# First attention and first mixture of experts: two steps of the sort a gap, the last sequence turned later, row fetches sent from an earlier step

## The chip, the cores and the metric

The kernel runs on one NeuronCore of one Trainium2 chip. The metric is the device time of one execution in microseconds (us), and the median over several executions is what counts. A profile of one execution gives the start and end of every instruction on the five engines (PE for matmuls, DVE for vector work, ACT for activations, POOL for GpSimd, SP for issuing transfers), and of every packet that the DMA engines moved.

## What is computed

The input is x with 8 sequences of 256 tokens and 256 features. Four layers follow each other, each an attention and a feed-forward part, and after each part x becomes layernorm(x + part(x)). Only the first layer matters here:

```python
def L0_attn(x):                       # 16 heads of 16, keys and values of 4 heads
    q, k, v = rope(x @ wq), rope(x @ wk), x @ wv
    return softmax(causal(q @ k.T / 4)) @ v @ wo

def L0_ffn(x):                        # 32 experts in 4 groups
    scores = sigmoid(x @ gate_w.T)
    two groups per token by the sum of their two best (scores + bias)
    the 8 best experts inside these two groups, weights scaled to sum 2.5
    h = relu((x @ fc1_w.T) @ w1[e].T) ** 2
    routed = sum over e of weight[e] * (h @ w2[e].T), then @ fc2_w.T
    shared = relu(x @ shared_up_w.T) ** 2 @ shared_down_w.T
    return shared + routed
```

Everything is float32 except a few 0/1 and mask operands in bf16.

## The kernel before, in words

The phases follow each other: attn0, ffn0, attn1 and so on. In attn0 and ffn0 the author writes the order of the instructions by hand: each engine's queue holds them in the order in which the Python generators issue them, apart from some that the recording layer of the manual schedule moves by a few places. [...]

**attn0** goes over the sequences b = 0 to 7. For each one it has three "gaps", i = 0, 1, 2: `maxima(b + 1)` makes a piece of the next sequence's scores (L331, mask L339) and takes their maxima on DVE (L343); `weights(b)` makes the transposed scores (L374, L382), ACT takes the exponentials (L388), and POOL clears the upper triangle of the diagonal blocks with an affine select (L390). After each of these comes a `fill(k, n)`. It runs what is ready beside the scores: pieces of `finish` (values L405, copy L410, transposes L416, division L420 and L421, transposes L431, copy L435, output projection L440, residual L164, statistics L183 and L184, reciprocal root on POOL L146 and L147, normalising L190), n pieces of the queue `ahead` (from b = 5 on the shared expert of token blocks 0 and 1, `ffn0_shared`, L1075 and L1088), and at its end one step of the queue `sorting`. `norm_done(b)` calls `transpose_x(b)` (L154), which turns the normalised X[b] into the block xT that all later matmuls read.

**The sort**, `ffn0_sort`, runs once for sequences 0 to 3 (group 0) and once for 4 to 7 (group 1). It is a generator of 23 steps and then 16 scatters. Step 1 to 3 gate and latent matmuls (L991, copies L995 on DVE and L996 on ACT), 4 sigmoid, 5 to 8 the best of each group (L1016), 9 the group choice (L1019 to L1022), 10 the one-hot `r_one` (L877, L879), 12 counting matmuls (L893) and their sums (L896 to L902), 13 and 14 slots, 15 and 17 which expert each tile has (L942, L944), 18 to 21 the best 8 experts (L230 to L235), 22 the weights, 23 their copy into the latent rows `lat` (L1054, L1060). Each scatter is one indirect transfer issued by POOL (L953), which writes 128 rows of 136 values to the table `lrows` in DRAM. POOL takes about a microsecond for each.

**ffn0** runs `ffn0_shared` for block 2 (sequences 4 and 5): eight steps, i = 0 to 3 for the four up-projections (two matmuls of 512 columns each, L1075), i = 4 to 7 for the down-projections (L1088). In its loop stand two sort steps per i, the turning of the last sequence, X[7], at i = 1, the start of group 1's sort at i = 4, and at i = 6 the first step of `ffn0_experts` and `then()`, which sends for the 6 MB of weights of attn1 on SP. `ffn0_experts` takes 19 tiles of 128 sorted rows. `fetch(j)` sends for the rows of tiles j and j + 1 (SP, L1110), `turn(j)` sends for the rows of tiles j + 4 and j + 5 if j is even, copies the tile's expert weights on POOL (`wc`, L1121) and transposes the rows (L1126, copy L1128 on ACT), `up` and `down` are the two matmul groups (L1134, L1151), with the weighted sum on DVE (L1160, L1162). During these tiles group 1's sort runs one step per half tile. The combine of group 0 and the tiles of group 1 follow in the same way, beside the shared expert of block 3.

PSUM has two buffers per tag (a, s, t, o). SBUF that attn0 used is given to ffn0 (weights `w2`, relu and hs, `wc`, `xg`) once attn0's last matmul has read it.

Of the kernel before, what the change touches and what calls it, by code (L numbers as in the profile page):

```python
# [19 lines left out]
NB = 8  # L20
# [19 lines left out]
class Model:  # L40
# [209 lines left out]
    def attn0(self, w, act, start=False, beside=None, between=()):  # L250
# [100 lines left out]
        def spread(b):  # L351

            pt = self.psum.tile([P, 2, P], BF16, tag="t", name="ps_tb")
            for qc in range(2):
                nc.tensor.transpose(
                    pt[:, qc, :], HLs[b % 2][:, qc].rearrange("p s r -> p (s r)"), self.identb
                )
            e = act.tile([P, 2, 4, P], BF16, tag="E", name="E")
            nc.vector.tensor_tensor(
                e,  # L360
                pt.unsqueeze(2).to_broadcast([P, 2, 4, P]),
                w["delta"].unsqueeze(1).unsqueeze(3).to_broadcast([P, 2, 4, P]),
                ALU.mult,
            )
            E[b] = e
# [96 lines left out]
        ends, ahead, sorting = [], [], []  # L462

        def step(queue):
            while queue:
                if next(queue[0], queue) is not queue:
                    return
                queue.pop(0)

        def fill(k, n):  # L470


            if k in (0, 2):
                for x in ends[-1:]:
                    next(x)
            if k == 0 and len(ends) > 1:
                next(ends.pop(0))
            for _ in range(n):
                step(ahead)
            if k in (3, 5):  # L480
                for x in ends[-1:]:
                    next(x)
            step(sorting)

        for _ in project(0):
            pass
# [5 lines left out]
        for b in range(NB):  # L492
            nxt = None
            if (b == 0 or b % 2 == 1) and (b + 3) // 2 < NBLK:
                ahead.append(project((b + 3) // 2))
            if b + 1 < NB:
                nxt = maxima(b + 1)
            if b == 0:
                steps = (3, 1, 1, 1, 1, 2)
            elif b % 2 == 1 and b < NB - 3:  # L500
                steps = (0, 2, 0, 1, 1, 1)
            elif b < NB - 3:
                steps = (0, 1, 0, 1, 1, 1)
            else:
                steps = (0, 1, 1, 1, 1, 1)
            if b == NB - 3:
                ahead.extend(between)
                if beside:
                    sorting.append(beside)
            mine = weights(b)  # L510
            for i in range(3):
                if nxt is not None:
                    next(nxt)
                if b > 1 and i == 1:
                    self.norm_done(b - 2)
                fill(2 * i, steps[2 * i])
                next(mine)
                if i == 2 and nxt is not None:
                    next(nxt, None)
                fill(2 * i + 1, steps[2 * i + 1])  # L520
            if nxt is not None:
                spread(b + 1)
            ends.append(finish(b))
# [574 lines left out]
    def ffn0_experts(self, w1, w2, g, act):  # L1098


        nc = self.nc
        rows, outs, expert = self.lrows[g], self.louts[g], self.sorted0[g][1]
        tiles = TILES0[g]
        xg, xT, h, er, wc, acc = {}, {}, {}, {}, {}, {}

        def fetch(j):
            if j < tiles:
                n = min(2, tiles - j)
                x = act.tile([P, 2, ROW0], F32, tag="xg", name="xg", bufs=4)
                nc.sync.dma_start(  # L1110
                    out=x[:, :n], in_=rows[j * P : (j + n) * P].rearrange("(n p) d -> p n d", p=P)
                )
                for i in range(n):
                    xg[j + i] = x[:, i, :]

        def turn(j):
            if j % 2 == 0:
                fetch(j + 4)
            e = nc.gpsimd.value_load(expert[0:1, j : j + 1], min_val=0, max_val=3)
            wc[j] = act.tile([P, 8, P], F32, tag="wc", name="wc", bufs=2)  # L1120
            nc.gpsimd.tensor_copy(  # L1121
                wc[j].rearrange("p e f -> p (e f)"),
                w1[:, bass.ds(e, 1), :].rearrange("p o f -> p (o f)"),
            )
            pt = self.ps("a")[:, :P]
            nc.tensor.transpose(pt, xg[j][:, :P], self.ident)  # L1126
            xT[j] = act.tile([P, P], F32, tag="xTg", name="xTg", bufs=3)
            nc.scalar.copy(xT[j], pt)  # L1128

        def up(s):  # L1130
            j, half = divmod(s, 2)
            ps = self.ps("s")
            for i in range(4):
                nc.tensor.matmul(  # L1134
                    ps[:, i * P : (i + 1) * P], wc[j][:, 4 * half + i, :], xT[j],
                    start=True, stop=True,
                )
            relu = act.tile([P, BLK], F32, tag="rl", name="rl", bufs=3)
            nc.scalar.activation(relu, ps, AF.Relu)
            h[s] = act.tile([P, BLK], F32, tag="hg", name="hg", bufs=3)  # L1140
            nc.scalar.activation(h[s], relu, AF.Square)

        def down(s):
            j, half = divmod(s, 2)
            if half == 0:
                er[j] = nc.tensor.value_load(expert[0:1, j : j + 1], min_val=0, max_val=3)
                acc[j] = act.tile([P, P], F32, tag="yg", name="yg", bufs=3)
            ps = self.ps("t")
            for i in range(4):
                k = (4 * half + i) * P  # L1150
                nc.tensor.matmul(  # L1151
                    ps[:, i * P : (i + 1) * P], h[s][:, i * P : (i + 1) * P],
                    w2[:, bass.ds(er[j], 1), k : k + P].rearrange("p o f -> p (o f)"),
                    start=True, stop=True,
                )
            for i in range(4):
                c = xg[j][:, P + 4 * half + i : P + 4 * half + i + 1]
                y = ps[:, i * P : (i + 1) * P]
                if half == 0 and i == 0:
                    nc.vector.tensor_scalar(acc[j], y, c, None, ALU.mult)  # L1160
                else:
                    nc.vector.scalar_tensor_tensor(acc[j], y, c, acc[j], ALU.mult, ALU.add)  # L1162
            if half == 1:
                nc.sync.dma_start(out=outs[j * P : (j + 1) * P], in_=acc[j])

        fetch(0)
        fetch(2)
        turn(0)
        yield
        for s in range(2 * tiles + 2):  # L1170
            if s < 2 * tiles:
                up(s)
            if s % 2 == 0 and s // 2 + 1 < tiles:
                turn(s // 2 + 1)
            if s >= 2:
                down(s - 2)
            yield
# [43 lines left out]
    def ffn0(self, w, act, keep, temp, sort, then, start=False):  # L1221

        w2 = self.load(act, "f0_w2", [P, 32, P], split=4)
        w1, w2 = (x.rearrange("p (g e) f -> p g (e f)", g=4) for x in (w["w1"], w2))
        if start:
            for b in range(NB):  # L1230
                self.transpose_x(b)
            for blk in range(2):
                for _ in self.ffn0_shared(w, blk, act):
                    pass
            sort = self.ffn0_sort(w, 0, temp, keep)
        tiles = self.ffn0_experts(w1, w2, 0, act)
        for i, _ in enumerate(self.ffn0_shared(w, 2, act)):
            next(sort, None)
            next(sort, None)
            if i == 1 and not start:  # L1240
                self.norm_done(NB - 1)
            if i == 4:
                for _ in sort:
                    pass
                sort = self.ffn0_sort(w, 1, temp, keep)
            if i == 6:
                next(tiles)
                then()
        for _ in tiles:
            next(sort, None)  # L1250
        for _ in sort:
            pass
        put = self.ffn0_combine(w, 0, keep)
        tiles = self.ffn0_experts(w1, w2, 1, act)
        for i, _ in enumerate(self.ffn0_shared(w, 3, act)):
            next(put, None)
            if i == 5:
                next(tiles)
        for _ in tiles:
            next(put, None)  # L1260
        for _ in put:
            pass
        return self.ffn0_combine(w, 1, keep)
# [1026 lines left out]
```

## Time and profile before

| What | us |
|---|---|
| median of 3 runs | 2521.76 |
| lowest and highest | 2521.01, 2522.95 |
| the profiled execution's own time | 2531.46 |
| its span, first to last instruction | 2529.7 |
| attn0 and ffn0's first half in it | 0 to about 393 |
| PE busy in the span | 2207.9 (87%) |
| DVE, ACT, POOL busy | 1431.1, 1046.2, 917.4 |

The profiled execution is 9.7 us (0.4%) longer than the median of the runs. All places in the text below, such as "at 280.5", are microseconds from the start of its span. A row of a timeline has the start, the length, the engine, the line, the operation, the tile written and the tiles read, the shapes and the count; at its end in brackets stands the time that the engine sat idle before it, and what ended that. A float32 matmul is two records, so one up-projection of 512 columns, two matmuls, is x4.

### The profile page before, as it was taken

To read this page: it belongs to the slowest core of one execution; us is meant where nothing else is said; L and a number is where in the kernel's file an instruction comes from. 1 tells how busy PE (TensorE), PEld (TensorE's weight loads), DVE (VectorE), ACT (ScalarE), POOL (GpSimd) and SP (SyncE) were. 2 spreads that over 40 slices of the span, in tenths; PEclk is the share of its full clock that TensorE was granted. 3 is DMA by queue.
4 is the path that set the end of the run, shared out by engine and by line. 5 is a ranking of instruction groups with operands and counts; after the bars stand their busy time and mean duration, and the time that the engine had idled before them with its cause. 6 is when DMAs were issued, how large, how long until landed. Compare 5 with 4: busy or idle time off the path is not lost. (4 is left out here: it accounts for less than half of the span.)

```text
span 2529.7 us, 36310 instructions
## 1 busy us (share of the span) xinstructions
PE 2207.9 (87%) x12016; PEld 1497.5 (59%) x12016; DVE 1431.1 (57%) x3593; ACT 1046.2 (41%) x3005; POOL 917.4 (36%) x1725
## 2 busy tenths in 40 slices
PE   7999789899999999999999999998878777678990
PEld 4454588756666666666664465555555554467780
DVE  4555486754544544544465454565888888645363
ACT  1334355553544544534431112121766755634440
POOL 1222443343433323333312321000566647824445
PEclk9999999999999999999999999999989988789995
DMA  5000411100000100000250011002000000155663
GB/s 159 1 1 1 157 48 40 53 14 4 4 3 3 52 1 1 1 1 1 81 197 0 1 50 51 1 0 102 1 2 1 1 1 28 38 139 174 200 203 96
DMA packets 92309, 120.76 MB, mean 48 GB/s; under 512 B 9757, under 2 KB 79582, under 8 KB 91102
## 3 DMA queue, kind: packets, MB, share of 16 engines
q1 hardware_dynamic: 82270, 95.75, 11.8%
q0 software_dynamic: 8192, 21.11, 2.8%
q8 instruction: 100, 1.64, 0.3%
q10 hardware_dynamic: 1664, 1.57, 0.2%
q14 instruction: 83, 0.68, 0.1%
HBM read 67.53 MB, written 50.88 MB: 47 GB/s over the span
## 5 line engine op out<-in xcount | busy, mean ns | idle before, releaser
L1388 POOL TENSOR_SCALAR p<-p,rs 128x128 f32<-128x128 f32 (+1 forms) x256 | 104.6, 428 | 293.7 <-DVE rs L1386 289.4
L1378 ACT ACTIVATE p<-ps_s,nm,rq 128x128 f32<-128x128 f32 (+1 forms) x256 | 128.0, 507 | 151.0 <-DVE nm L1376 151.0
L1306 ACT ACTIVATE sq<-ps_a 128x512 f32<-128x512 f32 x126 | 76.0, 603 | 228.1 <-PE ps_a L1298 225.9
L146 POOL TENSOR_SCALAR rsq<-bnmv 128x2 f32<-128x2 f32 x64 | 13.6, 213 | 385.4 <-DVE bnmv L184 377.8
L661 ACT ACTIVATE e<-ps_a,nm 128x128 f32<-128x128 f32 (+1 forms) x256 | 105.9, 435 | 108.9 <-DVE nm L658 95.4
L1307 DVE TENSOR_REDUCE ssk<-sq 128x4 f32<-128x512 f32 x64 | 43.8, 686 | 172.6 <-ACT sq L1306 172.6
L703 POOL TENSOR_SCALAR v<-e,r,nmd 128x128 f32<-128x128 f32 (+1 forms) x256 | 134.9, 540 | 10.0
L1298 PE MATMUL ps_a<-w_a_wq,xT 128*128 128x512 f32 x256 | 123.2, 604 | 12.1 <-DVE k L1320 9.2
L1978 PE MATMUL ps_a<-w_f_gup,xTg 128*128 x504 | 113.1, 349 | 12.8 <-DVE xTg L1972 5.5
L720 PE MATMUL ps_t<-ident,v 128*128 128x128 f32 x384 | 67.8, 312 | 62.3 <-DVE qT L599 30.6
L1298 PE MATMUL ps_a<-w_a_wv,xT 128*128 128x512 f32 x256 | 120.5, 593 | 1.0 <-ACT q L1331 1.0
L695 DVE SCALAR_TENSOR_TENSOR e<-e,c 128x128 f32<-128x128 f32 (+1 forms) x256 | 105.6, 462 | 23.0 <-POOL c L682 22.8
L1307 DVE TENSOR_REDUCE ssq<-sq 128x4 f32<-128x512 f32 x64 | 43.9, 686 | 131.0 <-ACT sq L1306 131.0
L1298 PE MATMUL ps_a<-w_a_wk,xT 128*128 128x512 f32 x248 | 116.5, 593 | 0.0
L1426 PE MATMUL ps_o<-w_a_wo,attT 128*128 128x256 f32 x512 | 111.8, 379 | 0.0
L661 ACT ACTIVATE e<-ps_s,nm 128x128 f32<-128x128 f32 (+1 forms) x256 | 106.8, 451 | 0.0
L1426 PEld LDWEIGHTS ps_o<-w_a_wo,attT 128*128 128x128 f32 x512 | 96.7, 190 | 12.8
L1162 DVE SCALAR_TENSOR_TENSOR yg<-ps_t,xg,yg 128x128 f32<-128x128 f32 x266 | 93.1, 350 | 13.8 <-PE ps_t L1151 3.5
L1365 PE MATMUL ps_s<-kT,qT 128*128 128x256 f32 (+1 forms) x512 | 99.5, 327 | 0.0
L1978 PEld LDWEIGHTS ps_a<-w_f_gup,xTg 128*128 128x128 f32 x504 | 83.3, 199 | 25.2 <-issue 10.5
L720 PEld LDWEIGHTS ps_t<-ident,v 128*128 128x128 f32 x384 | 49.4, 160 | 81.8 <-POOL nmd L700 29.9
L1412 PE MATMUL ps_o<-pT,V 128*128 128x256 f32 x256 | 79.5, 392 | 19.3 <-ACT pT L120 19.3
(410 smaller groups left out, 6072.7 us busy)
## 6 DMA issues: line engine op xcount, KB each, us to landing
rows<-zero SPq DMA_DIRECT2D x42, 384.0 KB
xg<-rows SPq DMA_DIRECT2D x42, 384.0 KB
outs<-yg SPq DMA_DIRECT2D x42, 384.0 KB
w_f_gup<-in_f_gup SPq DMA_DIRECT2D x8, 768.0 KB
w_f_w<-in_f_w SPq DMA_DIRECT2D x8, 512.0 KB
w_f_down<-in_f_down SPq DMA_DIRECT2D x8, 384.0 KB
w_f_up<-in_f_up SPq DMA_DIRECT2D x5, 512.0 KB
lrows<-zero SPq DMA_DIRECT2D x12, 204.0 KB
```

The source lines that it names most:

```text
L661: nc.scalar.activation(e[:, s, j * nk : (j + 1) * nk], sc[s][:, j, :], AF.Exp, bias=nm[:, s, j : j + 1], scale=1.0, accum_out=sums[:, s, j ...
L695: nc.vector.scalar_tensor_tensor(d[:, s, h, :], u.e[:, s, h, 1, :], u.c[:, s, h : h + 1], d[:, s, h, :], ALU.mult, ALU.add,)
L703: nc.gpsimd.tensor_scalar(u.v[:, s, h, :], d[:, s, h, :], u.r[:, s, h, 0:1], nm[:, s, h : h + 1], ALU.mult, ALU.add,)
L720: nc.tensor.transpose(ps[:, s, c, :], x, self.ident)
L1162: nc.vector.scalar_tensor_tensor(acc[j], y, c, acc[j], ALU.mult, ALU.add)
L1298: nc.tensor.matmul(ps, self.xt(u.b, t, c), w[which][:, c, u.cols], start=(c == 0), stop=(c == 1),)
L1307: nc.vector.tensor_reduce(out, sq, AX.X, ALU.add)
L1365: nc.tensor.matmul(sc[:, j, :], u.qT[:, h0 + j, qc * P : (qc + 1) * P], u.kT[:, h0 + j, 0:nk], start=(j == 0), stop=False,)
L1378: nc.scalar.activation(u.p[qc][:, h0 + j, :], sc[:, j, :], AF.Exp, bias=nm[:, j : j + 1], scale=r[:, j : j + 1], accum_out=u.sums[qc][:, h ...
L1388: nc.gpsimd.tensor_scalar(u.p[qc][:, j, :], u.p[qc][:, j, :], ri[:, j : j + 1], 1.0, ALU.mult, ALU.mult,)
L1426: nc.tensor.matmul(y[:, t, :], attTs[b][:, h, t * P : (t + 1) * P], w["wo"][:, h, :], start=(h == 0), stop=(h == 15),)
L1978: nc.tensor.matmul(ps, xT[j][:, c, :], w["gup"][:, bass.ds(er[j], 1), c, :].rearrange("p o f -> p (o f)"), start=(c == 0), stop=(c == 1),)
```

## The change

Five edits. `fill` takes two steps of the sort instead of one. The sort of group 0 joins the queue at b = 5 not ahead of the first gap but in the second one, behind `norm_done(3)`, so its first two steps come at the third `fill` of b = 5. In ffn0 the last sequence is turned at i = 3 instead of i = 1. `ffn0_experts` gets a `yield` between its first two fetches and `turn(0)`. In the first half of ffn0 these fetches and `then()` move to i = 4, `turn(0)` stays at i = 6; in the second half the fetches move from i = 5 to i = 3 and `turn(0)` stays at i = 5.

```diff
@@ attn0, in fill(k, n)
                 for x in ends[-1:]:
                     next(x)
             step(sorting)
+            step(sorting)
@@ attn0, loop over b
             if b == NB - 3:
                 ahead.extend(between)
-                if beside:
-                    sorting.append(beside)
             mine = weights(b)
             for i in range(3):
                 if nxt is not None:
                     next(nxt)
                 if b > 1 and i == 1:
                     self.norm_done(b - 2)
+                    if beside and b == NB - 3:
+                        sorting.append(beside)
                 fill(2 * i, steps[2 * i])
@@ ffn0_experts
         fetch(0)
         fetch(2)
+        yield
         turn(0)
         yield
@@ ffn0
         for i, _ in enumerate(self.ffn0_shared(w, 2, act)):
             next(sort, None)
             next(sort, None)
-            if i == 1 and not start:
+            if i == 3 and not start:
                 self.norm_done(NB - 1)
             if i == 4:
                 for _ in sort:
                     pass
                 sort = self.ffn0_sort(w, 1, temp, keep)
+                next(tiles)
+                then()
             if i == 6:
                 next(tiles)
-                then()
@@ ffn0, second half
         for i, _ in enumerate(self.ffn0_shared(w, 3, act)):
             next(put, None)
-            if i == 5:
+            if i in (3, 5):
                 next(tiles)
```

In the changed program the 16 scatters of group 0 stand on POOL as 7 ahead of the last four affine selects, 2 behind these and ahead of sequence 6's root, 7 behind that root; then come the two `wc` copies of tiles 0 and 1, and behind these the root of sequence 7. Before, 2 stood ahead of sequence 7's L146, 1 between its L146 and L147, and 13 behind. On PE the counting matmuls L893 stand in b = 6 behind the first gap's L1088 instead of behind L431 of the third. On SP `fetch(4)` stands behind attn1's weights instead of ahead of them. In ffn0's second half no queue's order differs.

## The prediction

> **What bounds the kernel now.** The busy shares come first: PE has 87% of the span, the next engine 57%. So the time is PE's, plus the holes in PE. The change touches 176 to 393 us only, so I took PE's timeline there and looked for idle brackets.
>
> ```profile
> 271.32 1.99 PE L440 MATMUL ps_o<-w_a_wo,aT 128*128 128x256 f32 x8 [1.35 <-DVE aT L435]
> 280.53 1.09 PE L154 MATMUL ps_t<-ident,X 128*128 128x128 f32 x4 [7.21 <-DVE X L190]
> 281.41 3.62 PE L1075 MATMUL ps_a<-xT,w_f_up 128*128 128x512 f32 x4
> 286.74 3.94 PE L1088 MATMUL ps_o<-w_f_down,hs 128*128 128x256 f32 x16
> ...
> 298.54 2.22 PE L991 MATMUL ps_a<-w_f_gate_fc,xT 128*128 128x160 f32 x8 [2.88 <-ACT lat L996]
> ...
> 303.67 1.13 PE L1134 MATMUL ps_s<-xTg,wc 128*128 128x128 f32 x8 [0.26 <-ACT xTg L1128]
> ```
>
> To be seen: from the end of attn0's last matmul (273.31) to the first expert matmul (303.67) 30.4 us pass. PE waits 7.21 us in front of the last sequence's transposes and 2.88 us for a copy of latent rows. The first L1075 behind the hole takes 3.62 us, elsewhere (at 186.96) 1.99.
>
> Next POOL's timeline, to see what X[7] waited for, and the table of waits:
>
> ```profile
> 274.86 1.43 POOL L953 DMA_INDIRECT lrows<-lat,r_slots  x1 [11.40 <-DVE lat L1060]
> 276.60 0.97 POOL L953 DMA_INDIRECT lrows<-lat,r_slots  x1 [0.30 <-issue]
> 277.64 0.19 POOL L146 TENSOR_SCALAR rsq<-bnmv 128x2 f32<-128x2 f32 x1
> 278.11 1.00 POOL L953 DMA_INDIRECT lrows<-lat,r_slots  x1 [0.28 <-issue]
> 279.14 0.74 POOL L147 TENSOR_TENSOR rstd<-rsq,nhalf 128x2 f32<-128x2 f32 x1
> ...
> 295.30 0.95 POOL L953 DMA_INDIRECT lrows<-lat,r_slots  x1 [0.30 <-issue]
> ```
> ```profile
> ACT lat L996 <- DMA lrows<-lat,r_slots: 9.5, 1, 9.5
> ```
>
> X[7]'s root stood among the scatters, and the scatters' end (296.3) set when ACT could write `lat` for group 1. Their pitch is 1.26 us (288.99, 290.25, 291.51). Last, the place where the sort's counting step will stand:
>
> ```profile
> 208.30 1.99 PE L440 MATMUL ps_o<-w_a_wo,aT 128*128 128x256 f32 x8 [0.71 <-ACT oS L410]
> ...
> 211.51 1.99 PE L1088 MATMUL ps_o<-w_f_down,hs 128*128 128x256 f32 x8
> ```
> ```profile
> 210.33 0.69 DVE L164 TENSOR_TENSOR res<-ps_o,X 128x512 f32<-128x512 f32 x1 [1.86 <-PE ps_o L440]
> ...
> 213.32 1.35 DVE L190 TENSOR_SCALAR X<-res,bnmv,rstd 128x256 f32<-128x256 f32 x2 [1.09 <-POOL rstd L147]
> ...
> 219.26 0.20 DVE L1019 TENSOR_TENSOR r_gs<-r_top 128x32 f32<-128x32 f32 x1
> ```
>
> **The change part by part.** Places are those of this trace; every cost is one of PE's path, and lines are the old ones.
>
> *Two steps a gap, b = 5.* The gate matmuls move by a few gaps; their PE time is the same (4.9 us). ACT's sigmoid comes 0.75 us later, so the maxima of the third gap do too; PE then waits 1.29 us for POOL's HL anyway (at 204.24), which hides it. Cost 0; without that cover 0.7.
>
> *b = 6, a new wait.* Steps 9 to 12 fall into one gap: group choice, `r_one`, counting. On DVE they stand behind the normalising of X[4]: L164 starts at 210.33 when L440 ends, L190 ends at 214.67, the choice takes 3.05 us (219.26 to 222.31 in its old place), `r_one` 0.4: ready at 218.05. On PE the counting matmul stands behind one weights group and L1088, which end at 213.50. PE waits 4.55 us, and behind it queue the scores L331, the transposes L154 of X[4], the values L405. L154 then needs the counts' PSUM buffer back: DVE adds X[0] (0.67) and sums (1.5), so it starts at about 220.3 against 215.28: 5.0 late. A gap of this size also costs clock. The last gap's maxima come another 1.1 us late, since the expert step (1.4 us of DVE, L1029 to L938) now stands ahead of them.
>
> *The clock.* The Trainium skill (TensorE: Matmul & The Clock Gate, "HAM oscillation") says that no PE gap over about 3.4 us should be left. The rows by windows differ from it: granted clock 0.75 and 0.82 in 232 to 240, with no gap there over 1.33 us, only three of 0.25, 0.33 and 1.33 around two tiny matmuls. By the rule the 4.55 us costs one half-speed window and the smaller gaps nothing. By the rows a stretch of 3.4 us with under about 45% of PE work costs one. For 4.55 us both say one window of 3.4, of which 1.1 to 3.4 us is work: 0.6 to 1.7 us lost, I take 0.8. For the gap of 1.6 us that remains before X[7]'s transposes the rule gives 0; the rows leave 53% busy, so also 0, but the end kept for the range is 1.7.
>
> *b = 6, an old wait goes.* L893 no longer stands behind L431: the brackets of 0.25, 0.33 and 1.33 go. Next late is POOL's HL (ends 232.38), so L355 starts at 232.45 against 233.64: 1.2. With them goes the low clock: L405 to the next L374 took 4.57 us (233.84 to 238.41), warm at 206.53 3.69: 0.9.
>
> *b = 7 and the tail.* DVE's steps 18 to 23 (1.3 + 1.7 + 2.0 us after X[5]'s L190 at 242.8) end at 247.8 and then the scatters start; DVE's next use is at 250.80, so they are hidden. In the tail DVE is free of the sort: the holes 1.17 (xT copy, 268.05) and 1.35 (above) go. Next late are PE's own matmuls. Gain 2.5; attn0 ends at 270.8 in old places.
>
> *Scatters on POOL.* Seven from 247.8 at 1.26: 256.7. Behind them the affine selects, ready at 255.0 before, end at 259.1 instead of 257.4; PE reads them at about 263.1, cover 4. Two more: 261.6; sequence 6's root can start at 262.4, cover 0.8. Seven more from 263.7: 272.5. Then `wc` twice (2.08): 274.6. Only then X[7]'s root, whose statistics are ready at 272.8: 1.9 late. Rows from 276.4.
>
> *X[7] turned later.* After 270.8 PE has two up-projections (2 x 1.9) to 274.6 and waits 1.5 to 1.6 for X[7]; transposes 0.6 (0.60 at 215.28); L1088 starts at 277.1. From attn0's end that is 6.3 us, before 13.43 (273.31 to 286.74): gain 7.1. relu and hs of the four blocks end at 275.9, no wait.
>
> *To the first expert matmul.* The scatters land about 274, long before `lat` is written (283). So 3.85 (L1088) + 3.3 (L991 x24) + 1.9 + 1.2 warm, then the chain of copy, table load, sigmoid, copy, 3.0 us (300.76 to 303.67 showed 2.9): 13.2 us against 16.9 (286.74 to 303.67): gain 3.7.
>
> *Fetches and weights on SP.* The fetches wait for the scatters (274), are queued behind `w2` (2 MB) and land about 278; first used at 287, so the earlier call is worth nothing by itself. SP now issues attn1's 6 MB from about 274; at the 364 to 437 GB/s of the DMA view at 304 to 318 they last 15 us, to 293. `fetch(4)` lands behind them, about 294; tile 4 is turned no earlier than 302: hidden, cover 8. Behind SP's waits stand only `fetch(6)` and the first stores of outputs. DVE's `gqk` product, which waited 1.09 us for the last of these loads at 318.50, no longer does, and PE waited for DVE there (2.37 at 321.24): gain 1.1. In ffn0's second half no queue changes: 0.
>
> Sum: gains 1.2 + 0.9 + 2.5 + 7.1 + 3.7 + 1.1 = 16.5; losses 5.0 + 0.8 + 1.1 = 6.9. Net 9.6 us. The profiled execution's 2531.46 (span 2529.7) would become 2521.9 (2520.1). It lies 9.7 us above the median; the difference in microseconds is carried to the median: 2521.76 - 9.6 = **2512**. Everything later is paced by PE and its own loads and shifts as a whole.
>
> **The rivals.** *Stalls of the doubled step eat most of it.* A second half-speed window behind the wait in b = 6 (1.7), one behind X[7]'s wait (1.7), the 0.7 of b = 5 not hidden, the 1.1 of `gqk` taken by another DVE step (+0.5 for the expert-number matmul waiting): 5.7 less, about 2518. For it: half windows follow quite small gaps here. Against it: each takes its own bad luck.
>
> *POOL becomes the bound (slower).* The Trainium skill warns (SBUF — State Buffer, "SBUF: two separate sides") that DVE can lock GpSimd out while it writes descriptors, 3.1 us for a transfer instead of 0.62. The rows: 32 scatters of 0.95 to 1.43 us, also at 352 to 378 where DVE is busy throughout; so 16 cost 20 us by the rows, 50 by the rule. At 3.1 the selects would be 9 us late, sequence 6's root 16, X[7]'s transposes some 28: net +18, about 2540. It turns slower than before above a pitch of about 1.9 us. The new place has DVE in the same kinds of operations, so I believe the rows.
>
> *The reordering does less harm than worked out*: part of PE's wait in b = 6 is made up by DVE work that is then already done, and no low clock follows: 3 to 5 more, about 2508 or below.
>
> *X[7] is not earlier*: its root sits behind `wc`, which needs attn0's SBUF. That is in the sum (1.9); only if `wc` waited for more than the last L440 would it grow, and `w2`, with the same release, started at 273.45, 0.14 after L440. X[7] as late as before would give back 4 us, about 2516; it is counted with the eaten case.
>
> **How the numbers follow.** Forecast 2512 (2508 to 2516.7): 0.66. Better (2504 to 2508): 0.10. Eaten (2516.7 to 2524): 0.15. POOL-bound (over 2527): 0.09. Faster by over 0.2% is below 2516.7, about what a measurement of this kernel can tell from no change: 0.76; within 0.2%: 0.15; slower: 0.09. The range 2506 to 2519 leaves out the slower case, half of the better and some 0.06 of the eaten one.
>
> **What would show it.** PE's timeline: a bracket of 4 to 5 us ahead of the counting matmul in b = 6, named DVE `r_one`; L355 waiting for POOL HL; no brackets ahead of the tail's L416 and L440; ahead of the last L154 one of 1 to 2.5 us instead of 7.21; none for `lat`; about 20 us from the last L440 to the first L1134. POOL: scatters from attn0's b = 7 at a pitch of 1.26, and X[7]'s root behind two `wc`. DVE: no wait at `gqk`. It is wrong if the pitch is over 1.5, if the wait in b = 6 is over 7 us, or if tile 4 waits for its rows.

## The result and the profile after

| | before | after |
|---|---|---|
| median of 7 runs each, us | 2522.95 (2521.01 to 2525.08) | 2514.54 (2511.68 to 2515.1) |
| ratio after / before | | 0.9965, 95% interval 0.9955 to 0.9975 |
| time of the profiled execution | 2531.46 | 2512.97 |
| attn1's first query projection (L1298, after L1301) starts at | 498.15 | 489.26 |

The change saves 8.4 us; the forecast was 9.6. The median of 2514.5 is 2.5 above the forecast 2512: half of that is the saving that is missing, half the kernel before, whose median over 7 runs is 1.2 us above the one that the forecast started from. The two profiled executions differ by 18.5 us, but only 8.9 of them lie ahead of attn1; the others lie in phases whose queues are the same in both programs, and the execution traced of before is 8.5 us above its own median. So places are compared up to attn1's start, and times by medians. One run of e1_one_step below, at 2562.31 us, fell in a slower state of the chip and is left out of its median.

PE's timeline of the kernel after, the rows that answer to those of before (line numbers are one higher here):

```profile
218.18 0.21 PE L894 MATMUL ps_t<-r_one,r_ones 128*128 128x32 bf16 x2 [4.88 <-DVE r_one L880]
...
221.23 1.06 PE L154 MATMUL ps_t<-ident,X 128*128 128x128 f32 x4
...
240.03 0.28 PE L355 MATMUL ps_tb<-identb,HL 128*128 128x128 bf16 x2 [1.14 <-POOL HL L349]
...
273.21 1.99 PE L440 MATMUL ps_o<-w_a_wo,aT 128*128 128x256 f32 x8
275.04 1.88 PE L1076 MATMUL ps_a<-xT,w_f_up 128*128 128x512 f32 x4
276.76 1.88 PE L1076 MATMUL ps_s<-xT,w_f_up 128*128 128x512 f32 x4
280.80 1.09 PE L154 MATMUL ps_t<-ident,X 128*128 128x128 f32 x4 [2.16 <-DVE X L190]
281.68 4.84 PE L1089 MATMUL ps_o<-w_f_down,hs 128*128 128x256 f32 x16
...
291.34 1.25 PE L992 MATMUL ps_a<-w_f_gate_fc,xT 128*128 128x160 f32 x8
...
295.50 1.13 PE L1135 MATMUL ps_s<-xTg,wc 128*128 128x128 f32 x8 [1.07 <-ACT xTg L1129]
```

To be seen are the new wait of 4.88 us in b = 6, the last L440 without a bracket, 2.16 us instead of 7.21 in front of the last sequence's transposes, no wait for `lat` ahead of the last L992, and 20.3 us from the last L440's end (275.20) to the first expert matmul instead of 30.4. What stands behind the 4.88 us in PE's queue comes late with it: X[4]'s L154 starts 13.1 us behind b = 4's L440 instead of 7.0. L1089 is slow: 4.84 us for what took 3.94 in before and takes 3.69 where the granted clock is 1.00 (in e8 below).

POOL's timeline of the kernel after:

```profile
252.07 1.23 POOL L954 DMA_INDIRECT lrows<-lat,r_slots  x1 [3.34 <-DVE lat L1061]
...
258.68 0.96 POOL L954 DMA_INDIRECT lrows<-lat,r_slots  x1 [0.30 <-issue]
259.94 0.95 POOL L954 DMA_INDIRECT lrows<-lat,r_slots  x1 [0.30 <-issue]
260.90 2.40 POOL L390 TENSOR_SCALAR_AFFINE_SELECT pT<-pT 128x512 f32<-128x512 f32 x4
...
276.13 0.96 POOL L954 DMA_INDIRECT lrows<-lat,r_slots  x1 [0.30 <-issue]
277.09 2.03 POOL L1122 COPY wc<-w_f_w 128x1024 f32 x2
279.20 0.19 POOL L146 TENSOR_SCALAR rsq<-bnmv 128x2 f32<-128x2 f32 x1
```

The scatters start in b = 7 at a pitch of 1.26 us (258.68 to 259.94) and are through at 277.09. X[7]'s root then stands behind two `wc` copies.

### The profile page after: what moved, and what is told of

Read it like the earlier page. It is cut to its first block, busy times and chain, and to the rows that moved or that the text cites. A ratio compares the mean times of both kernels' runs of the same rounds, so it can differ in the third digit from the quotient of the medians.

```text
span 2511.2 us, 36255 instructions
## 1 busy us (share of the span) xinstructions
PE 2192.5 (87%) x11960; PEld 1494.2 (60%) x12016; DVE 1431.1 (57%) x3593; ACT 1047.5 (42%) x3005; POOL 916.9 (37%) x1725
## 5 line engine op out<-in xcount | busy, mean ns | idle before, releaser
L146 POOL TENSOR_SCALAR rsq<-bnmv 128x2 f32<-128x2 f32 x64 | 13.6, 212 | 377.5 <-DVE bnmv L184 369.9
L1301 PE MATMUL ps_a<-w_a_wq,xT 128*128 128x512 f32 x256 | 122.3, 600 | 12.4 <-DVE k L1323 9.4
L1301 PE MATMUL ps_a<-w_a_wv,xT 128*128 128x512 f32 x256 | 120.6, 593 | 1.0 <-ACT q L1334 1.0
L1301 PE MATMUL ps_a<-w_a_wk,xT 128*128 128x512 f32 x248 | 116.5, 593 | 0.0
```

What stands on the lines that cost most here:

```text
L1301: nc.tensor.matmul(ps, self.xt(u.b, t, c), w[which][:, c, u.cols], start=(c == 0), stop=(c == 1),)
```

## The experiments

Three groups of kernels, each group on one chip beside its own runs of the kernel before. The chips differ by up to 13 us in that kernel, so medians are compared inside a group only. "Places" are starts in the trace, counted from b = 4's L440 (which starts at 206.5 to 209.0): the last L440, the last L154, the first expert matmul, attn1's first query projection.

| kernel | median | before, same chip | ratio, 95% interval | last L440 | last L154 | expert | attn1 |
|---|---|---|---|---|---|---|---|
| before | | | | 63.0 | 72.2 | 95.4 | 289.9 |
| after | 2514.54 | 2522.95 | 0.9965 (0.9955 to 0.9975) | 65.1 | 72.7 | 87.4 | 281.2 |
| e1_one_step | 2523.62 | 2534.90 | 0.9957 (0.9944 to 0.9970) | 64.3 | 73.2 | 89.2 | 283.6 |
| e2_root_first | 2519.72 | 2534.90 | 0.9945 (0.9932 to 0.9958) | 64.9 | 70.6 | 84.0 | 277.3 |
| e3_both | 2522.75 | 2534.90 | 0.9947 (0.9934 to 0.9960) | 64.5 | 71.3 | 84.8 | 278.2 |
| e4_single | 2535.51 | 2534.90 | 1.0003 (0.9995 to 1.0011) | 63.8 | 70.3 | 99.4 | 293.8 |
| e5_x7_i1 | 2525.54 | 2532.81 | 0.9975 (0.9964 to 0.9986) | 65.4 | 73.0 | 91.6 | 284.9 |
| e6_before_x7 | 2529.45 | 2532.81 | 0.9988 (0.9979 to 0.9996) | 63.2 | 73.0 | 95.1 | 289.3 |
| e7_fetch_late | 2521.05 | 2532.81 | 0.9960 (0.9947 to 0.9974) | 65.2 | 72.7 | 87.4 | 281.5 |
| e8_after_beside | 2512.73 | 2522.03 | 0.9968 (0.9955 to 0.9981) | 65.0 | 72.6 | 86.1 | 280.2 |
| e9_root_beside | 2508.55 | 2522.03 | 0.9947 (0.9933 to 0.9960) | 65.2 | 70.8 | 84.2 | 277.9 |
| e10_b6_single | 2513.94 | 2522.03 | 0.9965 (0.9951 to 0.9978) | 66.3 | 73.1 | 86.6 | 281.0 |
| e11_late_rest | 2507.99 | 2522.03 | 0.9942 (0.9929 to 0.9956) | 63.1 | 68.7 | 82.2 | 275.5 |

### Which part makes the gain

**One step a gap again.** `fill` ends with one `step(sorting)`, all else as after:

```diff
             step(sorting)
-            step(sorting)
```

> The changed kernel with one step of the sort a gap, as before; the later start of the sort, the last sequence turned at i = 3 and the earlier calls of the fetches stay. The scatters then begin after the sort's last steps in ffn0, near 278, and all 16 stand behind the last sequence's root. Theory (the gain comes from the scatters being done before ffn0 needs their buffer): no wait in b = 6's first gaps and a short one ahead of the last L154, but ACT's copy of lat waits until the scatters end near 298 to 300, the first expert matmul starts at 303 to 306: about as long as before, 2520 to 2524. Rival (the gain comes from turning the last sequence later and sending for rows sooner): 2512 to 2516.

The whole gain is gone, and the rows of POOL, ACT and PE show the theory's chain:

```profile
277.81 1.24 POOL L953 DMA_INDIRECT lrows<-lat,r_slots  x1 [1.59 <-DVE lat L1060]
...
297.05 0.95 POOL L953 DMA_INDIRECT lrows<-lat,r_slots  x1 [0.30 <-issue]
```
```profile
299.43 1.50 ACT L996 COPY lat<-ps_a 128x768 f32<-128x768 f32 x2 [21.32 <-DMA lrows<-lat,r_slots]
```
```profile
300.28 2.50 PE L991 MATMUL ps_a<-w_f_gate_fc,xT 128*128 128x160 f32 x8 [12.34 <-issue]
```

Though X[7] was turned sooner than in any kernel but e11, PE then stood 12.34 us. Its row names no releaser; ACT's does: `lat` is still being read by the scatters. By places e4 even loses 3.9 us against before, since the later start of the sort has stayed: its first scatter comes 71.3 us behind b = 4's L440, in before 66.6.

**The last sequence at i = 1 again** (`if i == 1 and not start`), as after otherwise:

> The changed kernel with the last sequence turned at i = 1 again, so that the last L154 stands ahead of two of the up-projections instead of behind all four. Theory (TensorE's order is what keeps it busy here): TensorE waits 5.3 to 5.6 us instead of 2.16, the two up-projections (3.8 us warm) follow at half clock: 4 to 5.5 us longer than the changed kernel, 2518.5 to 2520. Rival (the first expert tile is held by its rows, its weights or the sort, not by TensorE): within 1 us of the changed kernel.

```profile
282.00 1.09 PE L154 MATMUL ps_t<-ident,X 128*128 128x128 f32 x4 [5.58 <-DVE X L190]
282.88 3.24 PE L1076 MATMUL ps_a<-xT,w_f_up 128*128 128x512 f32 x4
...
296.44 1.25 PE L992 MATMUL ps_a<-w_f_gate_fc,xT 128*128 128x160 f32 x8
...
300.60 1.13 PE L1135 MATMUL ps_s<-xTg,wc 128*128 128x128 f32 x8 [1.07 <-ACT xTg L1129]
```

The wait is 5.58 us, and the first pair of up-projections behind it took 3.24 us. The median is 4.5 us above that of e7, which stands for after on this chip (by places 3.4): the theory held. But e5 is also the doubled step without the later turning, and it keeps most of the gain: L992 does not wait for `lat`, the first expert matmul comes 3.8 us sooner than in before, attn1 5.0, and the median is 7.3 us lower.

**That edit alone** (the kernel before with `if i == 3 and not start`):

> The kernel before, with the last sequence turned at i = 3 as the only edit. Theory (there the end of the scatters, near 296, lets ACT write lat and so sets the first expert matmul): the wait ahead of the last L154 falls from 7.2 to about 3.4 us, but the wait of L991 for lat grows from 2.9 to 6 to 7 us, and the time stays within 1 us of before, 2522 to 2523.5. Rival (the later turning is worth its 3.8 us by itself): 2518.5 to 2519.5.

```profile
280.93 1.08 PE L154 MATMUL ps_t<-ident,X 128*128 128x128 f32 x4 [6.15 <-DVE X L190]
281.81 5.32 PE L1088 MATMUL ps_o<-w_f_down,hs 128*128 128x256 f32 x16
...
297.67 2.50 PE L991 MATMUL ps_a<-w_f_gate_fc,xT 128*128 128x160 f32 x8 [5.55 <-ACT lat L996]
```

L1088 starts 4.6 us sooner than in before (281.81 - 207.94 against 286.74 - 208.30), the first expert matmul only 0.2 us: the wait for `lat` grew from 2.88 to 5.55, and the half clock took the rest. The wait ahead of L154 shrank less than expected, since part of the moved work filled the tail's hole of 1.35 ahead of L440 instead. The theory holds in the trace; the median is 3.4 us under before (interval 1.0 to 5.3), more than it says, and the trace shows no place for the rest. On this chip e5 and e7 too stand 2.3 and 3.4 us further below before than by places, so the rest need not come from this edit; it stays open. So the later turning needs the doubled step: alone it is worth 0.2 us at the first expert matmul, because the scatters still hold `lat`; on top of the doubled step (e7 against e5) it is worth 4.1 there. The reverse does not hold, as e5 shows.

**The fetch edits undone.** One call at i = 6 for the fetches, `turn(0)` and attn1's loads, in the second half at i = 5:

```diff
         fetch(2)
-        yield
         turn(0)
...
                 sort = self.ffn0_sort(w, 1, temp, keep)
-                next(tiles)
-                then()
             if i == 6:
                 next(tiles)
+                then()
...
-            if i in (3, 5):
+            if i == 5:
```

> The changed kernel with the calls of the fetches, of turn(0) and of the next attention's weights where they were before (one call at i = 6, in the second half at i = 5). On SP the only difference is that fetch(4) stands ahead of the next attention's weights again. Theory: 0 to 1.2 us longer, since only the loads' end moves. Rival A (the rows of tile 4, behind 6 MB of weights, hold TensorE where the trace shows 1.56 us ahead of its transpose): 0.5 to 1.5 us shorter. Rival B (sending for rows sooner is what moved the first expert tile): 3 us or more longer.

Places up to the first expert matmul are those of after, and attn1 starts 0.3 us later; no run tells that from nothing. SP's queue differs by one fetch, and its first fetches go out at 282.35 here, at 282.46 in after. Rival B falls: the first expert matmul did not move. Rival A falls by the trace: with tile 4's rows ahead of the weights, PE waits 1.54 us ahead of tile 4's transpose, in after 1.56, so the rows do not hold it. The medians say less, since after did not run on this chip and the two ratios' intervals overlap.

### The wait in b = 6

**The counting matmul one gap later:**

```diff
             step(sorting)
-            step(sorting)
+            if k not in single:
+                step(sorting)
...
+            single = {1} if b == NB - 2 else set()
             if b == NB - 3:
```

> The changed kernel, but the second fill of b = 6 takes one step of the sort instead of two, so that the counting matmuls stand one gap later on TensorE, behind the scores, the transposes of X[4] and the values; one scatter fewer stands ahead of the last affine selects. Theory (the 4.88 us wait for DVE's r_one and the two half-clock windows behind it, 215.9 to 222.7, are a real loss on the critical path): the wait is gone, L154 starts near 215.5 instead of 221.2, and some 1 us of the maxima's delay stays; 4.5 to 6.5 us less than the changed kernel's 2514.5, that is 2508 to 2510, ratio to before about 0.994. Rival (the wait only stands in for the maxima and HL behind it, which are late anyway because DVE does the sort): no more than 1 us less, 2513.5 to 2514.5.

The bracket went, and little was won: 0.8 us up to the last L440, and by places attn1 even starts 2.4 us later. The median, 11.3 us below before, cannot be set beside after's 8.4 from another chip. PE's timeline shows where the gain went:

```profile
218.53 1.99 PE L1091 MATMUL ps_o<-w_f_down,hs 128*128 128x256 f32 x8 [1.26 <-DVE X L1098]
...
221.51 0.20 PE L896 MATMUL ps_t<-r_one,r_behind 128*128 128x32 bf16 x2 [0.95 <-DVE xT L118]
...
233.34 3.78 PE L1078 MATMUL ps_t<-xT,w_f_up 128*128 128x512 f32 x4
```

The window rows of before, of after and of e1, in this order (columns: stretch, its length, then busy PE, PEld, DVE, ACT, POOL, the granted clock, DMA share, GB/s):

```profile
216.00:224.00 8.00, 8.00 (x58) 4.81 (x53) 7.06 (x39) 2.65 (x5) 0.14 (x1) 1.00 0.01 3
```
```profile
216.00:224.00 8.00, 5.82 (x44) 3.13 (x43) 7.21 (x34) 0.00 (x0) 0.00 (x0) 0.58 0.01 2
```
```profile
216.00:224.00 8.00, 5.79 (x41) 3.27 (x34) 7.31 (x35) 1.50 (x3) 0.00 (x0) 1.00 0.01 2
```

In after and e1 PE is busy 5.8 of the 8 us, and DVE 7.2 to 7.3. DVE's share alone shows no bound: in before it was 7.1, and PE did not wait. What differs is the order: the sort's group choice and `r_one` now stand ahead of the work that PE reads next (the shared expert's sum, a copy of xT), and PE waits for that instead. By places e1 is 6.2 us ahead of after at X[4]'s L154, 4.3 at the next L416, 2.9 at the L1078 shown and 1.1 at the L431 behind it. This last step is the clock: two half-clock stretches, 232.4 to 239.2, came in place of after's two (L1078 3.78 us instead of 1.98). And the sort came one step later: on POOL 8 scatters instead of 7 stood ahead of `wc` and X[7]'s root, and the wait ahead of the last L154 was 3.42 us instead of 2.16. The theory fell, and the rival's number was right; its reason, the maxima and HL late behind DVE's sort, is only a part of what the rows show.

**One step a gap through all of b = 6** (`single = set(range(6))`, on e2's kernel):

> The kernel of e2_root_first with one step of the sort a gap through all of b = 6, two again from b = 7. The counting matmuls stand in the second gap, 11 scatters ahead of the last sequence's root, 5 behind it. Theory (in b = 6 VectorE is near its bound: taking a wait away only moves it to the next reader of VectorE, but fewer sort operations there do make room): up to the last L440 1 to 2 us less than e2_root_first, but the root waits for 8 scatters that begin later, so ahead of the last L154 1 to 2 us more, and ACT's copy of lat waits up to 1 us: within 1.5 us of e9_root_beside. Rival (TensorE's own queue bounds b = 6): 4 us or more less up to the last L440.

Not 1 to 2 us less up to the last L440, but 1.1 to 1.4 more. DVE's sort work moved into b = 7, where PE meets it at the transpose of the tile numbers:

```profile
245.34 0.27 PE L948 MATMUL ps_t<-ident,r_te 128*1 128x128 f32 x1 [3.42 <-DVE r_te L944]
```

Both the theory and its rival fell, and the median is 5.4 us above e9's. What remains is that sort work has to fit between DVE's own steps; no run here says beforehand which split does.

### The last sequence's root

**The residual and root issued at the start of ffn0**, so that on POOL they stand ahead of `wc`:

```diff
-            r = self.residual(b, y)
-            self.normed(b, r, *self.moments(r))
+            if b == NB - 1 and not self.last:
+                self.late = y
+            else:
+                r = self.residual(b, y)
+                self.normed(b, r, *self.moments(r))
             yield
...
+        if not start:
+            r = self.residual(NB - 1, self.late)
+            self.normed(NB - 1, r, *self.moments(r))
         tiles = self.ffn0_experts(w1, w2, 0, act)
```

> The changed kernel, but the residual, statistics and root of the last sequence are issued at the beginning of ffn0 instead of at attn0's end, so that on POOL its root stands ahead of the two wc copies; nothing else moves. Theory: rstd is ready at about 278.1 instead of 280.2, the wait of 2.16 us ahead of the last L154 shrinks to 0.3 to 0.6 and the half-clock window 280.7 to 284.1 behind it goes too: 2 to 3.5 us less than the changed kernel, 2511 to 2512.5. Rival A: the low clock there does not come from this gap and stays: 1.7 us less only. Rival B: the wc copies, now 1 us later, or the rows set the start of the first expert tile: no difference.

```profile
277.12 0.19 POOL L146 TENSOR_SCALAR rsq<-bnmv 128x2 f32<-128x2 f32 x1 [0.15 <-DVE bnmv L184]
277.39 0.72 POOL L147 TENSOR_TENSOR rstd<-rsq,nhalf 128x2 f32<-128x2 f32 x1
```
```profile
278.71 0.67 PE L154 MATMUL ps_t<-ident,X 128*128 128x128 f32 x4 [0.19 <-DVE X L190]
279.47 3.69 PE L1092 MATMUL ps_o<-w_f_down,hs 128*128 128x256 f32 x16
```

The wait is 0.19 us, L1092 runs at full clock, and the first expert matmul comes 3.4 us sooner than in after. The theory held. Beside after on one chip:

> The changed kernel itself, once more, so that it stands beside the next three on one chip. Theory (the gain over before is the 8.7 us of the first attention and ffn that its trace shows, whatever the chip): 8 to 11 us less than before, ratio 0.9957 to 0.997. Rival (a part of its gain lies in later phases and differs from chip to chip): 12 us or more less, or under 6.

> The kernel of e2_root_first once more, beside the changed kernel on one chip. Theory (the wait of 2.16 us and the half-clock windows behind it and beside tile 5 go, 3.9 us up to the next attention's first projection by the traces): 3 to 5 us less than the changed kernel in this call. Rival (the two traces differ by chance, the times do not): within 1.5 us of it.

4.2 us less, as expected (by places 2.3 to 3.9). And after is 9.3 us below before on this chip, 8.4 on the first.

**e1 and e2 together:**

> The two edits of e1_one_step and e2_root_first together. Theory: their gains add, since they lie 60 us apart and nothing between them is paced by another thing than TensorE: 7 to 9.5 us less than the changed kernel, 2505 to 2508. Rival (a common bound behind both, e.g. the end of the scatters or the loads of the next attention): not more than the larger of the two.

They do not add: by places attn1 starts 0.9 us later than in e2 alone, because an eighth scatter stands ahead of the root (1.41 us of wait ahead of the last L154). The median is 3.0 us higher, but the runs overlap. The common bound is POOL's queue.

**Rest of the scatters behind the root**, on e2's kernel: `single = {0, 1}` in b = 6 and `{3, 5}` in the tail:

> The kernel of e2_root_first with one step of the sort in the first two fills of b = 6 and in the last two of the tail; 3 scatters then stand behind the last sequence's root, and the counting matmuls behind the values as in e1_one_step. Theory: no bracket at the counting matmul, two smaller ones for VectorE behind it and one half-clock window as in e1_one_step, 0.5 to 1 us less up to the last L440; the root is not held by scatters, the wait ahead of the last L154 stays under 0.6 us: 0.3 to 1.2 us less than e9_root_beside. Rival (e3_both showed that the two edits disturb each other): 0.5 us or more longer than it.

The last L440 comes 1.8 to 2.1 us sooner than in e2 and e9, twice what was expected; the wait ahead of the last L154 is 0.18 us. At 2507.99 us it is the fastest, 14.0 us below before, but against e9's 2508.55 the runs do not separate it: the two intervals overlap. Both e9 and e11 beat before; against after, e9's and e11's runs (2506.7 to 2511.3) all lie below after's (2511.4 to 2515.7).

## Why the prediction was right

**By its steps.**

| step | forecast, us | measured |
|---|---|---|
| b = 5 at no cost, HL wait as cover | 0 | 1.10 of 1.29 left |
| wait at counting, b = 6 | 4.55 | 4.88 |
| up to L355 of b = 6 (losses 5.0, 0.8, 1.1; gain 1.2) | 5.7 later | 6.6 later |
| from there to the last L440, gain (0.9, 2.5) | 3.4 | 4.5 |
| net up to the last L440 (losses 5.0, 0.8, 1.1; gains 1.2, 0.9, 2.5) | 2.3 later | 2.1 later |
| pitch, root of sequence 6 | 1.26, cover 0.8 | 1.26, POOL itself waits 1.43 |
| wait ahead of the last L154 | 1.5 to 1.6 | 2.16 |
| L440 to L1088/L1089, gain | 7.1 | 6.95 (15.42 to 8.47) |
| L1088/L1089 to first expert matmul, gain | 3.7 | 3.1 (16.93 to 13.82) |
| first expert matmul to attn1 (`gqk`), gain | 1.1 | 0.7 (194.5 to 193.8) |

Sum 6.95 + 3.1 + 0.7 - 2.1 = 8.7, the 8.7 us of the places; the medians say 8.4. Of the signs named for being wrong none came: the pitch was 1.26 us, the wait in b = 6 under 7, and tile 4 did not wait for its rows (e7).

**Mis-sized terms.** That the net up to the last L440 fits is in part luck: the way to L355 came out 0.9 us too short, the way behind it gave 1.1 us more than was counted. In b = 6 there was not one stretch of 3.4 us at half clock but two (215.9 to 222.7), and L154 took 1.06 us instead of 0.60. Behind X[7]'s wait the sum took the clock at 0, with 1.7 as the bound: the granted clock was 0.59 in 280 to 284, and L1089 took 4.84 us where the sum had 3.85. In e8, the same program, the clock was 1.00 there and L1089 took 3.69. On SP the first fetches went out at 282.46, later than the 278 at which they were to have landed; they were covered all the same.

**Right result, incomplete reason.** The 4.88 us were priced as PE's loss. e1 shows that removing the bracket gives back only 0.8 us: PE then waits for DVE's next results, and the half-clock stretches come later. The sum was right because it also counted what DVE no longer did later (1.2 + 0.9 + 2.5); it would have misled whoever went after the bracket. The gains of 7.1 and 3.7 were given one by one, to the turning and to the scatters. That of the scatters stands by itself (e5: 3.8 us at the first expert matmul without the later turning). That of the turning does not: in e6 4.6 us of it are there at L1088, and 0.2 at the first expert matmul.

**The rivals.** *POOL-bound*: the pitch stayed at 1.26 us in after while DVE was busy 5.50 of 8.76 us (268.33 to 277.09). The stretch of 352 to 378 that the prediction rests on had DVE busy 19.8 of 26 us, not throughout. e4's 16 scatters in 20.2 us say nothing on it: DVE was busy 2.0 us of them. *Stalls eat most*: of its four prices a second window in b = 6 and one behind X[7] did come, and part of the gain at `gqk` stayed out; e8 shows that the one behind X[7] may also stay away. *Less harm*: no low clock was its condition, and it did come. *X[7] not earlier*: its transposes start 0.5 us later by places, but behind four up-projections; its root behind `wc` came 2.0 us late as priced (by places, after against e2), but it was worth 2.3 to 3.9 us by places and 4.2 by medians to remove (e9), since the clock behind the wait came on top in after's trace.

## What to carry to other kernels

Before giving each wait its price, look for the second wait that ends at nearly the same place: an edit may be worth nothing until another one has taken that wait away. A bracket on PE says who came last, not that removing it pays; follow the order of work on the engine that it names, because the busy share there was the same with the wait and without it. And when work is moved onto a queue, read what else stands in it: one scatter (1.26 us) or two copies (2.03) ahead of a small root (0.9) hold up everything that waits for the root.

## What was unexpected of the hardware

A PE gap of about 2 us may or may not be followed by a stretch at half clock. The window rows of the same instructions with the same wait of 2.16 us, in after and in e8, and PE's rows in e8:

```profile
280.00:284.00 4.00, 3.20 (x10) 2.74 (x11) 0.73 (x2) 0.66 (x2) 0.20 (x1) 0.59 0.83 309
```
```profile
280.00:284.00 4.00, 3.40 (x17) 2.86 (x18) 0.59 (x2) 0.59 (x1) 0.00 (x0) 1.00 0.81 289
```

```profile
280.42 0.67 PE L154 MATMUL ps_t<-ident,X 128*128 128x128 f32 x4 [2.16 <-DVE X L190]
281.27 3.69 PE L1089 MATMUL ps_o<-w_f_down,hs 128*128 128x256 f32 x16 [0.18 <-PE ps_t L154]
```

Half clock followed waits of 2.00 us (e4) and 2.16 (after, e7), but not of 2.16 (e8), 1.41 (e3) and 1.38 (e10). The kept traces show what tells most of them apart. In each of the 13 the stretches at half clock start only at multiples of 3.41 us from one another, on a grid that lies differently in every run. So a wait can fall into one slot of the grid or across two. In the slot with the wait PE was busy 1.34 of 3.42 us in after (from 277.30) and 1.45 of 3.41 in e4 (from 274.95), and the next slot ran at half clock; in e8 it was 1.47 of 3.42 (from 276.78), in e3 1.92 (from 277.22), and the next slot ran at full clock. In b = 6 of after the 4.88 us left PE 25% and 32% busy in two slots running, and two slots at half clock followed.

Counted from 150 to 500 us over all traces, a full-clock slot with PE busy up to 44% was followed by half clock in 34 of 35 cases (the other is e8's, 43%), and one with 46% or more stayed at full clock in 1235 of 1238 (the others, 88 to 90%, are in e1, e3 and e11). So the prediction's 45% held in this part of the kernel; where a wait would fall on the grid could not be foretold. Behind 500 us the border is less sharp. The Trainium skill's rule (TensorE: Matmul & The Clock Gate, "HAM oscillation"), gaps over about 3.4 us, is too kind for these traces. Why e8's slot at the border and the three busy ones went the other way stays open.
